# Who issues the stores of rectified chunks: GpSimd in place of SyncE in two passes of a Fourier-layer kernel

## The chip, the cores and the metric

The kernel runs on one core of one Trainium2 chip. The metric is the device time of one execution in microseconds (us). Five runs of the kernel before gave a median of 11392.32 us (11384.97 to 11395.28). The profile is of one further execution, whose own time was 11374.28 us.

## The reference

The model is a tokenizer followed by one transformer layer, for 64 images of 256 x 256 points, all in float32. The tokenizer is a Fourier neural operator with four layers over 32 channels:

```python
v = concat([x, gx, gy]) @ p_w + p_b                  # 3 -> 32 channels
for i in range(4):
    x1 = irfft2(W_i * rfft2(v) on 24 x 12 low modes)   # mixes channels per mode
    x2 = einsum('bcxy,cd->bdxy', v, w_w[i]) + w_b[i]
    v = x1 + x2
    v = (v - mean) * rsqrt(var + 1e-5) * bn_g[i] + bn_b[i]   # statistics over batch, x and y
    if i < 3:
        v = relu(v)
h = squeeze(v @ q_w + q_b)                            # 64 x 256 x 256
h = concat([h, txt], axis=1)                          # 333 tokens of 256
h = h + attention(layernorm(h)); h = h + routed_ffn(layernorm(h))
```

The mean and variance of a layer are over the whole batch, so no image's v can be rectified until the layer's statistics are complete for all 64 images. One full v is 64 images x 8 MiB and does not fit on the core, so it lives in HBM.

## The kernel before

The program has these stages, one after the other: `forward_first` (the low modes of the first v, straight from x), then for each layer i a short stage `mix(i)` (channel mixing per mode, batch statistics), and after the first three of them a long pass `layer(i)`, i = 0, 1, 2. The last layer and the transformer are the tail.

A pass `layer(i)` makes the next v, image by image, in 8 chunks per image. A chunk is a tile of 128 partitions x 8 rows x 256 values, 8 KiB per partition and 1 MiB in all. Its steps are small functions, and each is named by a word:

- `ld` (L632 to L636, passes 1 and 2 alone): loads the chunk of the old v into a tile `vin`, as two halves of 512 KiB (128 partitions x 4 KiB). There are 4 buffers of `vin`. Pass 0 computes its old v from x and loads none.
- `pre`: TensorE adds the inverse transform (L662) and the product of the weights with `vin` (L673) in PSUM (`ring`, four tiles of two banks).
- `evA`, `evB`: each rectifies half of the chunk from PSUM into the tile `vo`, on ScalarE (L685) or VectorE (L687). There are 4 buffers of `vo`.
- `st` (L691 to L694): stores `vo` to HBM, again as two halves of 512 KiB. This is the step that the change touches.
- `turn` (L699) transposes `vo` on VectorE, `prod` (L710) multiplies it by the next layer's weights, and `sqA`, `sqB` (L721) sum squares of that on ScalarE. A `vo` buffer is free for the chunk four later when its store has landed and `turn` and `prod` have read it.
- once per image: `am` loads the mixed modes (`ams`, L603, SyncE's queue) and scales them in place on GpSimd (L611); `sp` and `spT` start the inverse transform from them (L642, L650); `y0` to `y7` (L732), `half`, `zt`, `x` (L766), `xo` make the forward transform of the finished image, and `xs` (L783) stores its modes.

The order is written out by hand. `ORDER` has one string for pass 0 and one for passes 1 and 2: a list of words, each with a chunk number, `@` and an offset of the image, and `.a` or `.d` for the evicting engine. The function `layer` walks through the list once per image and issues the steps under a manual schedule, so each engine gets its instructions in just this order and waits at the first one that is not ready. For passes 1 and 2 it is:

```python
"pre5 sqB7@-1 zt1@-1 sqA7@-1 pre6 evA5.a ld2@1 st4 evB5.d st5 turn4 evA6.a prod5 x@-1 "
"evB6.a sqB5 prod6 sqA5 xo@-1 turn5 pre2@1 sqA6 turn6 sqB6 prod4 evA2.a@1 evB2.d@1 "
"sqB4 ld0@1 ld7 sqA4 pre0@1 evB0.d@1 ld3@1 prod2@1 st6 evA0.a@1 turn2@1 sqB2@1 sqA2@1 "
"pre3@1 ld1@1 evA3.a@1 st2@1 evB3.d@1 pre7 evB7.d prod3@1 ld5@1 evA7.a sqA3@1 turn7 "
"pre1@1 st0@1 am@2 sqB3@1 prod0@1 evA1.a@1 evB1.d@1 sqA0@1 st7 sp1@1 st1@1 ld4@1 y0 "
"spT1@1 y1 ld6@1 turn0@1 turn3@1 xs@-2 y2 sqB0@1 prod1@1 y3 sqB1@1 sp0@2 y4 sqA1@1 "
"spT0@2 y5 y6 st3@1 turn1@1 y7 half.a pre4@1 zt0 prod7 evB4.d@1 evA4.a@1 "
```

Read for one queue alone, this gives SyncE the order ld2, st4, st5, ld0, ld7, ld3, st6, ld1, st2, ld5, st0, am's load, st7, st1, ld4, ld6, xs, st3. GpSimd has in these passes only the scaling of `am`. Where a pass ends, GpSimd issues the next layer's weight loads (`wn`, L387) and the large load of the modes (`xh`, L826).

Of the kernel before, what the change touches and what calls it, by code (L numbers as in the profile page):

```python
# [153 lines left out]
def tile_fno_fusion_transformer(ctx: ExitStack, tc: tile.TileContext, a, cst_d, grid_d, out):  # L154
    nc = tc.nc
# [370 lines left out]
    def layer(i, st, src, dst, acc):  # L526
# [7 lines left out]
        with ExitStack() as cx:  # L534
# [64 lines left out]
            y_, t32, vin, vo, half_, zts = {}, {}, {}, {}, {}, {}  # L599
# [91 lines left out]
            def st_(b, t, e):  # L691
                for n in range(2):
                    rows = slice(4 * n, 4 * n + 4)
                    nc.sync.dma_start(dst[b][:, t, rows], vo[b, t][:, rows])  # L694

            def turn(b, t, e):
                if (b, t // 2) not in t32:
# [84 lines left out]
            def xs(b, n, e):  # L782
                nc.sync.dma_start(xh_d[i][:, b, :], xos.pop(b).rearrange("p g k -> p (g k)"))  # L783

            run = dict(
                am=am, lx=lx, ld=ld, sp=sp, spT=spT, pre=pre, evA=ev(0), evB=ev(1), st=st_, turn=turn,
                prod=prod, sqA=sq(0), sqB=sq(1), y=y, half=half, zt0=zt(0), zt1=zt(1), x=x_, xo=xo, xs=xs,
            )
# [143 lines left out]
    rows = [128, 128, TXT]  # L932
# [283 lines left out]
```

## Time and profile before

| | |
|---|---|
| median of 5 runs | 11392.32 us |
| profiled execution: time, span | 11374.28 us, 11372.5 us |
| granted TensorE clock, mean | 0.976 |
| busy over the span: PE, DVE, ACT, POOL | 93%, 74%, 57%, 13% |
| pass 0, 250 to 2700 us: DMA share, GB/s | 0.71, 248 |
| pass 1, 2900 to 5600 us: DMA share, GB/s | 0.98, 376 |
| pass 2, 5900 to 8500 us: DMA share, GB/s | 0.98, 379 |
| tail, 8900 to 11372 us: DMA share, GB/s | 0.55, 216 |

PE is TensorE's matmuls, DVE VectorE, ACT ScalarE, POOL GpSimd, SP SyncE; SPq and POOLq are the instruction queues from which SyncE and GpSimd issue DMAs. The DMA share is the mean busy share of the core's 16 DMA engines; since packets of different queues can overlap in the records, it can pass 1 for a moment. In the profile a wait is put down to what ended it, and the time "to landing" of a DMA is from its issue to its completion signal, time spent behind other transfers included.

### The profile page before, as it was taken

The numbers are of one execution on the slowest core, as the hardware profiler recorded it, in microseconds if no ns is written. First come the engines' busy times: TensorE is split into PE (matmuls) and PEld (weight loads), VectorE is DVE, ScalarE is ACT, GpSimd is POOL, SyncE is SP. The second block draws the span as 40 slices with busy tenths as digits, with TensorE's granted clock in tenths as the row PEclk, the third lists the DMA queues.
The fourth block names the chain that finished last, engine by engine and source line by source line (L and its number), as shares of the span: only waits on it lengthen the run. The fifth ranks groups of instructions, "written<-read, shape, count | busy, mean of one in ns | idle before, by whom it ended". The sixth has DMA issues, their size and how long they took to land. (4 is left out here: it accounts for less than half of the span.)

```text
span 11372.5 us, 408517 instructions
## 1 busy us (share of the span) xinstructions
PE 10577.0 (93%) x182038; PEld 5726.4 (50%) x182038; DVE 8461.7 (74%) x10405; ACT 6494.3 (57%) x10697; POOL 1477.9 (13%) x2243
## 2 busy tenths in 40 slices
PE   6999999997999999999699999999995999999998
PEld 3555555543444444444344444444443666666666
DVE  6888888886777777777677777777775666666665
ACT  5777777775656656665556665565653333333333
POOL 0111111110000000000100000000001333333333
PEclk7999999998999999999899999999997999999999
DMA  7676676769999999999899999999998555555553
GB/s 235 247 249 245 246 250 247 249 235 327 380 384 380 382 381 376 377 382 381 294 374 384 384 381 378 379 376 376 385 374 272 225 228 228 225 226 227 229 227 135
DMA packets 977151, 3485.52 MB, mean 306 GB/s; under 512 B 151320, under 2 KB 200856, under 8 KB 905368
## 3 DMA queue, kind: packets, MB, share of 16 engines
q1 hardware_dynamic: 906880, 3376.23, 77.6%
q0 software_dynamic: 61360, 79.44, 3.1%
q8 instruction: 1424, 23.33, 0.8%
q10 hardware_dynamic: 7144, 3.72, 0.1%
q14 instruction: 343, 2.81, 0.1%
HBM read 1761.87 MB, written 1696.92 MB: 304 GB/s over the span
## 5 line engine op out<-in xcount | busy, mean ns | idle before, releaser
L721 ACT ACTIVATE ring<-ring 128x1024 f32<-128x1024 f32 x3072 | 3115.9, 1014 | 1178.8 <-PE ring L710 1112.1
L699 DVE STREAM_TRANSPOSE t<-vo 128x2048 f32<-128x2048 f32 x1536 | 3465.4, 2286 | 20.8 <-DVE vo L687 0.5
L710 PE MATMUL ring<-vo,w 32*32 32x512 f32 x49152 | 2404.0, 599 | 82.3 <-ACT vo L685 66.8
L687 DVE TENSOR_SCALAR vo<-ring 128x1024 f32<-128x1024 f32 x1280 | 1545.4, 1222 | 1178.1 <-PE ring L673 801.7
L685 ACT ACTIVATE vo<-ring 128x1024 f32<-128x1024 f32 x1792 | 1791.8, 1023 | 1029.1 <-PE ring L673 489.8
L732 PE MATMUL ring<-t,cst 32*32 32x512 f32 x49152 | 2067.7, 599 | 46.5 <-issue 39.8
L732 PEld LDWEIGHTS ring<-t,cst 32*32 32x32 f32 x49152 | 912.2, 103 | 919.2 <-issue 613.3
L710 PEld LDWEIGHTS ring<-vo,w 32*32 32x32 f32 x49152 | 802.6, 103 | 1062.0 <-issue 397.2
L611 POOL TENSOR_TENSOR ams<-ams,bns 48x512 f32<-48x512 f32 x384 | 401.4, 1045 | 6956.2 <-DMA ams<-mix 6732.7
L662 PE MATMUL ring<-cst,y 24*128 24x256 f32 x16384 | 1228.6, 402 | 74.9 <-DVE vo L687 60.1
L673 PE MATMUL ring<-vin,ws 32*32 32x512 f32 x32768 | 1276.5, 602 | 16.8 <-issue 12.5
L662 PEld LDWEIGHTS ring<-cst,y 24*128 24x128 f32 x16384 | 788.1, 185 | 988.9 <-DVE vo L687 389.6
L650 DVE STREAM_TRANSPOSE y<-ring 128x1024 f32<-128x1024 f32 x384 | 762.9, 1987 | 324.4 <-PE ring L642 323.3
L662 PE MATMUL ring<-mv,y 29*128 29x256 f32 x8192 | 704.2, 403 | 37.2 <-ACT ring L721 19.5
L662 PEld LDWEIGHTS ring<-mv,y 29*128 29x128 f32 x8192 | 455.9, 185 | 368.8 <-ACT ring L721 207.4
L766 PEld LDWEIGHTS ring<-cst,zt 128*128 128x128 f32 x4608 | 532.1, 193 | 178.0 <-ACT vo L685 114.4
L742 ACT COPY half<-ring 128x1024 f32<-128x1024 f32 x192 | 194.4, 1013 | 725.4 <-PE ring L732 725.4
L1165 POOL DMA_DIRECT2D out_dram<-o x1024 | 510.9, 507 | 658.1 <-DVE o L1160 616.5
L721 ACT ACTIVATION_READ_ACCUMULATOR ring<-ring 128x1 f32 x3072 | 585.3, 191 | 0.0
L766 PE MATMUL ring<-cst,zt 128*128 128x96 f32 x4608 | 564.1, 279 | 7.6 <-DVE zt L750 7.2
L750 DVE STREAM_TRANSPOSE zt<-ring 128x1024 f32<-128x1024 f32 x192 | 377.3, 1965 | 242.2 <-PE ring L732 242.2
L642 PE MATMUL ring<-ams,cst 49*128 49x512 f32 (+1 forms) x1536 | 451.8, 642 | 104.3 <-POOL ams L611 38.0
(367 smaller groups left out, 9804.1 us busy)
## 6 DMA issues: line engine op xcount, KB each, us to landing
v<-vo SPq DMA_DIRECT2D x3072, 512.0 KB, 7.8
vin<-v SPq DMA_DIRECT2D x2048, 512.0 KB, 9.1
ch<-v SPq DMA_DIRECT2D x512, 1024.0 KB, 12.7
mix<-ob SPq DMA_DIRECT2D x96, 512.0 KB, 5.7
ams<-mix SPq DMA_DIRECT2D x384, 96.0 KB, 7.9
xin<-in_x_dram SPq DMA_DIRECT2D x16, 1024.0 KB, 6.0
mv<-in_x_dram POOLq DMA_DIRECT2D x256, 64.0 KB, 7.1
out_dram<-o POOLq DMA_DIRECT2D x1024, 16.0 KB, 3.0
```

Source lines behind the costliest of these rows:

```text
L642: nc.tensor.matmul(ps[:, n, :], lhsT=EX[hv, 128 * h:128 * h + 128], rhs=ams[b % 2][hv], start=True, stop=True, skip_group_check=True,)
L650: nc.vector.transpose(y_[b, h].rearrange("p q c -> p c q"), ring[key][0][1].rearrange("p n (c k) -> p (n c) k", k=32),)
L662: nc.tensor.matmul(ps[n][:, 256 * r:256 * r + 256], lhsT=y_[b, t // 4][32 * n:32 * n + K, q:q + 4, :].rearrange("p q c -> p (q c)"), rhs=m ...
L673: nc.tensor.matmul(ps[n][32 * j:32 * j + 32], lhsT=ws[32 * n:32 * n + 32], rhs=v[32 * n:32 * n + 32, 2 * j:2 * j + 2, :], start=False, sto ...
L685: nc.scalar.activation(to, ring[key][h][1], AF.Relu)
L687: nc.vector.tensor_scalar(to, ring[key][h][1], 0.0, None, ALU.max)
L699: nc.vector.transpose(t32[b, t // 2][:, :, 8 * (t % 2):8 * (t % 2) + 8, :].rearrange("p y s c -> p s y c"), vo[b, t].rearrange("p s (y l) ...
L710: nc.tensor.matmul(ps[n][32 * j:32 * j + 32], lhsT=w4[i + 1][32 * n:32 * n + 32], rhs=vo[b, t][32 * n:32 * n + 32, 2 * j:2 * j + 2, :], st ...
L721: nc.scalar.activation(ps, ps, AF.Square, accum_out=acc[:, at:at + 1])
L732: nc.tensor.matmul(ps[n][32 * j:32 * j + 32], lhsT=FYT[32 * n:32 * n + 32, k, :], rhs=t32[b, j][32 * n:32 * n + 32, k].rearrange("p s c -> ...
L766: nc.tensor.matmul(ps[:, 0, 96 * g:96 * g + 96], lhsT=zt_[:, h, k0:k0 + 4, :].rearrange("p k c -> p (k c)"), rhs=FX[:, h, 48 * r:48 * r + ...
L1165: nc.gpsimd.dma_start(out[b, 64 * n + 16 * g:64 * n + 16 * g + 16].rearrange("(p t) d -> p t d", t=2), o[32 * g + 8 * n:32 * g + 8 * n + 8 ...
```

## The change

In passes 1 and 2 (where `i` is not zero) the two half-chunk stores of `st` are issued from GpSimd's queue. In pass 0 they stay with SyncE. The loads `ld`, am's load and `xs` stay with SyncE in all passes. `ORDER`, buffers, sizes and addresses are as they were.

```diff
             def st_(b, t, e):
                 for n in range(2):
                     rows = slice(4 * n, 4 * n + 4)
-                    nc.sync.dma_start(dst[b][:, t, rows], vo[b, t][:, rows])
+                    (nc.gpsimd if i else nc.sync).dma_start(dst[b][:, t, rows], vo[b, t][:, rows])
```

## The prediction

> **What bounds the kernel now.** I read the page's 40 slices first, to see in which stage which resource is full.
>
> ```profile
> PEclk7999999998999999999899999999997999999999
> DMA  7676676769999999999899999999998555555553
> GB/s 235 247 249 245 246 250 247 249 235 327 380 384 380 382 381 376 377 382 381 294 374 384 384 381 378 379 376 376 385 374 272 225 228 228 225 226 227 229 227 135
> ```
>
> Slices 10 to 29 are passes 1 and 2, the only ones that the change touches: DMA stands at 9 tenths or more. The table by stretches of the two passes is sharper (columns: PE, PEld, DVE, ACT, POOL busy; clock; DMA share; GB/s), and the DMA view of the first of them counts the transfers.
>
> ```profile
> 3000.00:5500.00 2500.00, 2399.22 (x51319) 1132.35 (x51306) 1884.92 (x1052) 1508.29 (x2375) 115.06 (x110) 1.00 0.99 380
> 6000.00:8500.00 2500.00, 2394.89 (x51248) 1135.95 (x51251) 1879.83 (x1050) 1509.32 (x2381) 115.03 (x110) 1.00 0.98 379
> ```
>
> ```profile
> vin<-v SPq DMA_DIRECT2D x884, 512.0 KB, 9.1
> v<-vo SPq DMA_DIRECT2D x884, 512.0 KB, 8.8
> ```
>
> 884 half stores are 55.25 images of 16, so an image takes 2500 / 55.25 = 45.2 us. TensorE is busy 2399 / 55.25 = 43.4 us of it and idle 1.8 us. Two resources are nearly full, DMA and TensorE, and neither is quite full. A half chunk at 380 GB/s takes 1.4 us; a store that takes 8.8 us to land has spent most of that behind others. The waits of the same 2500 us, first of SyncE's queue, then of the engines:
>
> ```profile
> SPq L694 <- ACT vo L685: 441.4, 113, 7.3
> SPq L694 <- DMA v<-vo: 296.0, 329, 2.4
> ```
>
> ```profile
> POOL ams L611 <- DMA ams<-mix: 2367.3, 55, 44.7
> ACT vo L685 <- DMA v<-vo: 123.6, 90, 2.7
> DVE vo L687 <- DMA v<-vo: 118.3, 92, 3.1
> ```
>
> So twice per image (113 / 55) SyncE stands 441.4 / 113 = 3.9 us before a store whose chunk is not rectified yet, and whatever loads are behind it stand too. And rectifying waits (123.6 + 118.3) / 55.25 = 4.4 us per image for an old store to land, since its buffer is not free. The order in time of SyncE's queue in one image, and DMA in stretches of 2 us of it:
>
> ```profile
> 4086.80 5.36 SPq L694 DMA_DIRECT2D v<-vo  x4
> 4092.26 3.60 SPq L636 DMA_DIRECT2D vin<-v  x6
> ```
>
> ```profile
> 4086.00:4088.00 2.00, 1.74 (x47) 0.72 (x16) 2.00 (x2) 1.91 (x4) 0.00 (x0) 1.00 0.48 193
> 4088.00:4090.00 2.00, 2.00 (x52) 0.97 (x48) 1.52 (x2) 1.55 (x3) 0.00 (x0) 1.00 1.02 403
> 4090.00:4092.00 2.00, 2.00 (x66) 0.92 (x68) 2.00 (x2) 0.80 (x2) 0.00 (x0) 1.00 0.52 195
> ```
>
> The four half stores are st4 and st5. Until st5 is out at 4092, the six half loads of ld0, ld7, ld3 stand, and the engines run half empty twice: 2 x (0.52 + 0.48) = 2.0 us lost. One image earlier (stretches from 4040 to 4048: 0.91, 1.01, 0.72, 0.91) it is 0.9 us. The mean, 1.45 us per image, is what can be filled.
>
> **The change part by part.**
>
> *Stores leave SyncE.* 2 passes x 64 images x 16 = 2048 DMAs go. The loads behind them issue when a `vin` buffer is free: ld0 needs the buffer that pre5 reads, which ends near 4089.4, three us before its issue at 4092.26. That is the size of the dips. A store also no longer lands behind up to three chunks of loads, so part of the 4.4 us of waiting for `vo` goes. Late next is TensorE, with only 1.8 us of idle time. Gain per image: at least 0 (the dips only move), at most 1.8. I take half of the mean dip, 0.73 us, since stores and loads still share the same engines in the dense half of the image; 0.73 x 128 images = 93 us.
>
> *Stores join GpSimd.* The page's GpSimd rows give the price of an issue:
>
> ```profile
> L618 POOL DMA_DIRECT2D mv<-in_x_dram x256 | 146.6, 576 | 632.2 <-PE ring L662 531.2 <-DVE ams L564 81.3 <-issue 13.5
> L826 POOL DMA_DIRECT2D xh<-xh x3 | 1.7, 566 | 1.9 <-DMA wn<-in_L_tok_fw_dram 1.9
> ```
>
> 16 x 0.57 = 9.1 us per image beside 115 / 55.25 = 2.1 us of scaling: 11.2 of 45.2, hidden in GpSimd's idle time. If it were not hidden it could cost at most the difference to SyncE's 0.32 us at the last chunk of a pass, 0.5 us each.
>
> *Stores queue behind am's wait.* GpSimd now meets st0, then the scaling, which waits for `ams` (8.7 us median to land, then 2.1), then st7, st1, st3. For up to 10.8 us no store can issue. The chunks next rectified are 1, 4, 5, 6; by fours they reuse the buffers of 2, 0, 3, 7. Only 5 and 6 need stores behind the wait, and y0 to y7 (L732, some 11 us of TensorE) lies before them. Cost 0; without that cover up to 10.8 us per image, and below nothing not, since the wait starts nothing earlier. SyncE reaches am's load sooner (st0 no longer before it), so `sp0`, which needs the scaling, is not later.
>
> *The end of a pass.* The next layer's weight loads (L387) stand on GpSimd behind the last two half stores: 2 x 0.57, for 2 passes 2.3 us. With the 1 us above: 3 us.
>
> *Two queues at the engines.* No row shows full-size loads and stores from both. GpSimd's large load alone (4 MB, no other traffic) ran at the engines' full rate:
>
> ```profile
> 5595.00:5604.00 9.00, 0.00 (x0) 0.00 (x0) 1.25 (x2) 1.32 (x2) 1.84 (x4) 0.50 1.04 431
> ```
>
> The other end is pass 0, where GpSimd's 64 KB loads meet SyncE's stores: from 1022 to 1024 the share was 1.05 at 275 GB/s, from 1010 to 1012, without them, 1.02 at 404. Those loads go to 4 partitions each, so they are far from a 128-partition store; the large load is nearer, and I take 0. Ends kept: 431 against 380 would be hidden by TensorE's limit (the 1.8 us); 275 against 404, a third less, would cost about 2000 us.
>
> The sum: -93 + 3 = -90 us. The profiled execution took 11374 us, so 11284; the median of the runs lies 18 us above it: 11302, say 11300.
>
> The row of 0.48 and 0.52 stands against a rule of the Trainium skill. "DMA: Bandwidth & Descriptors", section "Issuing engines are not separate DMA queues", says that all issuers share the same 16 engines and that a second issuer saves only the issue time at the sequencer. By the rule the sum would be about 0 and the time 11392; by the row it is -90, because what SyncE loses is not issue time but waiting in order. The page "SBUF — State Buffer", section "SBUF: two separate sides", speaks against the change too: GpSimd cannot write its descriptors while VectorE runs in a 2-port mode; the VectorE rows of these passes (2283 ns for 2048 values, 1224 for 1024) show about one value per ns, so no doubled rate, and I take no loss from it.
>
> **The rivals.**
>
> *More: TensorE becomes the bound.* If decoupling removes dips and buffer waits wholly, an image takes 43.4 us: 1.8 x 128 = 230 us, 11160. For it: SyncE's 8 us of standing per image. Against: DMA then needs 17 MB in 43.4 us, 395 GB/s, and its best stretches show 400 to 415.
>
> *Same: the dips only move.* The loads go out earlier, land earlier and wait; the engines run dry later in the image, when no buffer is free. 11392, within 23 us (0.2%, about what a measurement of this kernel can tell from no change). For it: the DMA share is already 0.98 to 0.99.
>
> *Slower: packets of two queues get in each other's way.* Loads and stores now alternate at each engine packet by packet. The spare is 1.45 of 45.2 us, 3.2%; from a loss of rate over that it decides. A sixth of the loss seen in pass 0 (a third) is 5.5% of 43.4, or 2.4 us; less the 1.45 filled, +0.95 x 128 = +120 us: 11510. For it: the 275 GB/s row. Against: the 431.
>
> **How the numbers follow.** The forecast (a fill of about half) 0.40, more 0.17, same 0.13, slower 0.30. Faster 0.57, same 0.13, slower 0.30. The likeliest one's own range is 11220 to 11365 (fill of nearly all the dip down to a fifth of it). The 8-in-10 range reaches to TensorE's bound, 11150, and on the other side over half of the slower case, to 11470.
>
> **What would show it.** Right: SyncE's waits at L694 in passes 1 and 2 gone, those for `vin` readers in their place; the dips at st4 and st5 filled; `v<-vo` landing in under 8.8 us from POOLq; "vo <- DMA v<-vo" well below 242 us per 2500; DMA at 385 GB/s or more. Wrong: the same share with fewer GB/s (packets slower); GpSimd's wait for `ams` followed by rectifying that waits for stores; TensorE waiting for `vin` at L673, because loads now share with stores.

## The result and the profile after

The changed kernel took 11369.43 us (median of 25 runs, 11352.93 to 11383.05) beside 11388.43 us for the kernel before (43 runs). The ratio is 0.9984 with a 95% interval of 0.9978 to 0.9989. The gain is 19 us by the medians and 18 us by the ratio (13 to 25). That is a real gain, of the sign forecast, a fifth of the size forecast, and by its middle value within the 0.2% that the prediction called no change, though the interval reaches just past it. The forecast of 11300 us is 69 us too low, and the likeliest case's own range (to 11365) ends 4 us short of the time; the wide range holds it. The profiled execution took 11358.6 us, with a span of 11356.8 us and a granted clock of 0.976, as before.

First the windows of the two passes after the change (columns as in the prediction: PE, PEld, DVE, ACT, POOL busy; clock; DMA share; GB/s), and the DMA view of the first of them.

```profile
3000.00:5500.00 2500.00, 2400.85 (x51311) 1140.32 (x51314) 1885.70 (x1050) 1514.91 (x2385) 581.72 (x996) 1.00 0.98 380
6000.00:8500.00 2500.00, 2402.52 (x51348) 1143.86 (x51342) 1887.81 (x1051) 1512.15 (x2378) 583.88 (x998) 1.00 0.98 380
```

```profile
q1 hardware_dynamic: 142464, 479.19, 51.3%
q0 software_dynamic: 127380, 463.85, 46.1%
vin<-v SPq DMA_DIRECT2D x886, 512.0 KB, 10.3
v<-vo POOLq DMA_DIRECT2D x886, 512.0 KB, 10.2
```

Almost nothing in the first fence moved but POOL. DMA still carries 380 GB/s, and TensorE is still busy 2401 of 2500 us. In the second fence the traffic has become two queues of equal weight, and a store now takes longer to land (10.2 us for 8.8), not less.

The waits of the same window, SyncE's queue and then the engines:

```profile
SPq L636 <- PE ring L673: 1472.3, 381, 13.7
SPq L636 <- DMA vin<-v: 320.6, 210, 3.6
```

```profile
POOL ams L611 <- DMA ams<-mix: 544.7, 52, 12.2
DVE vo L687 <- DMA v<-vo: 106.4, 74, 3.4
ACT vo L685 <- DMA v<-vo: 71.9, 60, 2.4
PEld ring L673 <- DMA vin<-v: 0.7, 2, 0.6
```

SyncE's waits at L694 are gone. It now stands 1472 us of 2500 before a load whose `vin` buffer TensorE is still reading (L673), and 321 us more are put down to an earlier load: no load stands behind a store any more, and the buffers set when most of them go out. GpSimd carries the stores' waits instead:

```profile
POOL v L694 <- ACT vo L685: 1319.0, 330, 12.8
```

Where the dry stretch went is seen in one image of pass 1, in stretches of 2 us, and in the two issuing queues around it:

```profile
4074.00:4076.00 2.00, 2.00 (x65) 0.93 (x68) 1.70 (x2) 0.84 (x2) 0.00 (x0) 1.00 0.68 270
4076.00:4078.00 2.00, 1.74 (x47) 0.72 (x16) 2.00 (x2) 1.91 (x4) 0.53 (x1) 1.00 0.66 145
4078.00:4080.00 2.00, 2.00 (x52) 0.97 (x48) 1.53 (x2) 1.55 (x3) 0.00 (x0) 1.00 0.97 299
```

```profile
4060.00 20.63 SPq L636 DMA_DIRECT2D vin<-v  x6
```

```profile
4063.05 3.21 POOL L694 DMA_DIRECT2D v<-vo  x6
4077.03 0.53 POOL L694 DMA_DIRECT2D v<-vo  x1 [10.76 <-ACT vo L685]
```

From 4066 to 4077 GpSimd has nothing to store, because during `y0` to `y7` TensorE makes no new chunk, so nothing new is rectified. The six half loads of SyncE take 20.6 us to issue for the same reason: no chunk is consumed, so no `vin` buffer comes free. When both have run out, the engines fall to 145 GB/s. Averaged over the middle images of pass 1, GB/s in stretches of 2 us from `sp1`, counted from the trace's packet records:

```
us from sp1   0   2   4   6   8  10  12  14  16  18  20  22  24  26  28  30  32  34  36  38  40  42  44
before      412 412 413 413 415 411 409 414 343 354 267 331 309 297 378 386 357 395 393 411 406 410 414
after       411 405 407 414 413 416 413 342 153 262 331 383 319 354 415 413 415 412 410 416 417 411 411
```

The shallow loss from 16 to 38 us has become a deep one from 14 to 28 us, of the same area: the mean rate is 380 GB/s in both. The equal area shows no more than that an image takes about as long as before, since the bytes are the same. And the deep stretch is no wait of TensorE: its weight loads for L673 waited 0.7 us of 2500 for `vin` (the last row of the waits above), against 12.5 us before.

Last, how long an image takes. The table gives the interval from one image's `sp1` on TensorE to the next one's, in passes that ran the full work (two of before, two of after, and passes of the experiments below). "First" is the first interval of a pass, "later" the mean of the other 62.

| stores of the pass | passes | first, us | later, us (each) | later, mean |
|---|---|---|---|---|
| SyncE, four vin, four vo | 5 | 39.3 to 39.9, mean 39.6 | 45.20, 45.29, 45.43, 45.43, 45.41 | 45.35 |
| GpSimd, four vin, four vo | 4 | 36.6 to 39.0, mean 37.6 | 45.18, 45.24, 45.31, 45.16 | 45.22 |
| the same, `half` moved (see the experiments) | 2 | 38.3, 38.3 | 45.34, 45.14 | 45.24 |
| GpSimd, four vin, five vo | 2 | 36.1, 38.3 | 45.15, 45.21 | 45.18 |
| SyncE, five vin | 2 | 39.7 to 39.9, mean 39.8 | 45.46, 45.36 | 45.41 |
| GpSimd, five vin | 4 | 37.6 to 38.4, mean 38.2 | 45.08, 45.10, 45.17, 45.14 | 45.12 |

The profiled executions of before and after alone (45.20 and 45.29, 45.18 and 45.24) show scarcely any gain per image, since before's was one of its quicker ones; and of the 15.7 us between their two spans, 9.2 lie ahead of the first `sp1` of pass 1, where the change does nothing. Over all the passes of the first two rows the gain is 0.13 us for a later image and 2.0 us for the first: 2 x (62 x 0.13 + 2.0) = 20 us, which agrees with the 18 us measured. The split is rough: the passes of one kind differ by up to 0.23 us for a later image and 2.4 us for the first.

The 2 us at the start of a pass can be seen directly. SyncE's queue where pass 1 begins, before:

```profile
2655.64 4.12 SPq L636 DMA_DIRECT2D vin<-v  x8
2667.60 0.80 SPq L694 DMA_DIRECT2D v<-vo  x2
2668.49 1.98 SPq L636 DMA_DIRECT2D vin<-v  x2
2670.57 9.42 SPq L694 DMA_DIRECT2D v<-vo  x4
```

and after:

```profile
2646.70 48.76 SPq L636 DMA_DIRECT2D vin<-v  x26
```

Before, the fifth chunk's load stood behind the first store of the pass (2667.60), and the next two behind stores that took 9.4 us to issue. After, the first 26 half loads follow one another with no store between them.

### The profile page after: what moved, and what is told of

The parts are those of the page before. It is cut to its first block, busy times and chain, and to the rows that moved or that the text cites. A ratio compares the mean times of both kernels' runs of the same rounds, so it can differ in the third digit from the quotient of the medians.

```text
span 11356.8 us, 408660 instructions
## 1 busy us (share of the span) xinstructions
PE 10568.4 (93%) x182038; PEld 5737.3 (51%) x182038; DVE 8468.0 (75%) x10405; ACT 6499.2 (57%) x10697; POOL 2553.3 (22%) x4291
## 5 line engine op out<-in xcount | busy, mean ns | idle before, releaser
L710 PE MATMUL ring<-vo,w 32*32 32x512 f32 x49152 | 2432.5, 599 | 51.7 <-ACT vo L685 34.2
L732 PE MATMUL ring<-t,cst 32*32 32x512 f32 x49152 | 2099.1, 599 | 60.3 <-issue 53.6
L694 POOL DMA_DIRECT2D v<-vo x2048 | 1086.8, 535 | 3135.7 <-ACT vo L685 3077.9
L732 PEld LDWEIGHTS ring<-t,cst 32*32 32x32 f32 x49152 | 919.4, 103 | 956.4 <-issue 641.2
L710 PEld LDWEIGHTS ring<-vo,w 32*32 32x32 f32 x49152 | 817.6, 103 | 1024.4 <-issue 447.5
L662 PE MATMUL ring<-cst,y 24*128 24x256 f32 x16384 | 1225.4, 401 | 110.3 <-DVE vo L687 85.9
L662 PEld LDWEIGHTS ring<-cst,y 24*128 24x128 f32 x16384 | 784.0, 184 | 1025.3 <-DVE vo L687 421.0
L673 PE MATMUL ring<-vin,ws 32*32 32x512 f32 x32768 | 1235.6, 601 | 10.3 <-issue 10.0
L662 PE MATMUL ring<-mv,y 29*128 29x256 f32 x8192 | 705.0, 403 | 37.0 <-ACT ring L721 20.1
L662 PEld LDWEIGHTS ring<-mv,y 29*128 29x128 f32 x8192 | 455.9, 185 | 369.0 <-ACT ring L721 211.6
## 6 DMA issues: line engine op xcount, KB each, us to landing
vin<-v SPq DMA_DIRECT2D x2048, 512.0 KB, 10.2
```

The costliest lines, as they stand in the source:

```text
L662: nc.tensor.matmul(ps[n][:, 256 * r:256 * r + 256], lhsT=y_[b, t // 4][32 * n:32 * n + K, q:q + 4, :].rearrange("p q c -> p (q c)"), rhs=m ...
L673: nc.tensor.matmul(ps[n][32 * j:32 * j + 32], lhsT=ws[32 * n:32 * n + 32], rhs=v[32 * n:32 * n + 32, 2 * j:2 * j + 2, :], start=False, sto ...
L694: (nc.gpsimd if i else nc.sync).dma_start(dst[b][:, t, rows], vo[b, t][:, rows])
L710: nc.tensor.matmul(ps[n][32 * j:32 * j + 32], lhsT=w4[i + 1][32 * n:32 * n + 32], rhs=vo[b, t][32 * n:32 * n + 32, 2 * j:2 * j + 2, :], st ...
L732: nc.tensor.matmul(ps[n][32 * j:32 * j + 32], lhsT=FYT[32 * n:32 * n + 32, k, :], rhs=t32[b, j][32 * n:32 * n + 32, k].rearrange("p s c -> ...
```

## The experiments

Two theories stood against each other at first. By one, DMA and its dry stretches hold the image: with less to move it falls to TensorE's 43.4 us, and the change gained little because it filled little. By the other, TensorE's order with its hand-overs holds it: transfers that start earlier, or fewer of them, move it little. The letters A, B and so on belong to each expectation as it words them. Every kernel below starts from before or from the changed kernel, as its diff says.

### Less to store, stores on SyncE

```diff
-                for n in range(2):
+                for n in range(1 if i == 2 else 2):
```

> The kernel before (all stores on SyncE), but pass 2 stores only the first half of each chunk: 512 of its 1024 half stores, a quarter of its traffic, are left out; pass 1 is as it was and serves as control. Theory A (an image is held by its transfers, as the prediction's sum had it): pass 2's image falls from 45.2 us to TensorE's busy time of 43.4, the whole by some 115 us to 11275. Theory B (TensorE's order of work with its hand-overs to the evicting engines holds the image at 45.2, and transfers have room in it): pass 2's image stays within 0.3 us of 45.2, the whole within 25 us of the kernel before.

Measured, one execution of each: 11327.2 us beside 11403.37 on the same chip. A later image of pass 2 took 44.30 us, and of the untouched pass 1 45.43. Pass 2's window:

```profile
6000.00:8300.00 2300.00, 2228.62 (x48180) 1085.81 (x48176) 1772.83 (x987) 1423.64 (x2233) 108.69 (x104) 1.00 0.81 293
```

With a quarter of the traffic gone the DMA share falls to 0.81, yet the image loses only some 1.1 us, between the fall to 43.4 us and the standstill that were expected. TensorE still stands 2300 - 2229 us over 2300 / 44.3 images, 1.4 us per image, of the 1.8 us that it stood before. So most of the idle time on which the forecast drew is not DMA's: it lies in hand-overs that lighter DMA leaves as they are. The rest of the 1.1 us came out of TensorE's busy time, which fell to 2229 / 51.9 = 42.9 us per image, so the 43.4 us of the prediction are no fixed floor.

### The same with stores on GpSimd

```diff
-                for n in range(2):
+                for n in range(1 if i == 2 else 2):
                     rows = slice(4 * n, 4 * n + 4)
                     (nc.gpsimd if i else nc.sync).dma_start(dst[b][:, t, rows], vo[b, t][:, rows])
```

> The changed kernel with only the first half of each chunk stored in pass 2 (the other half is not written, so DMA there has a quarter less to move); stores on GpSimd in passes 1 and 2. Theory A (an image is held by TensorE's order with its hand-overs, some 44.3 us once DMA is light, whichever engine issues the stores): pass-2 image 44.3 us, as when SyncE issued the halved stores. Rival D (GpSimd's issue itself slows the work, which is why the steady image gained nothing): over 44.7 us. Rival E (SyncE's waits cost TensorE something even with light DMA): 43.4 to 43.9 us.

Measured, in one execution: 11299.56 us beside 11386.91. A later image of pass 2 took 44.10 us.

```profile
6000.00:8300.00 2300.00, 2225.61 (x48369) 1075.92 (x48368) 1779.71 (x991) 1426.77 (x2242) 329.21 (x520) 1.00 0.81 294
```

Theory A held: 44.1 us with GpSimd as issuer, 44.3 with SyncE, not 43.4. Under light DMA an image ends near 44.2 us whoever issues the stores; a gain as small as the 0.13 us of the change can't be told apart here, as the two single executions differ by 0.2 us. A quarter less traffic brings some 1.1 us per image, so a change of issuer, which moves as many bytes as before, could hardly have brought 0.73.

### Less for TensorE, then both, then with the change

The y steps 1 to 6 go in pass 2; the second kernel takes the halved stores of the first experiment as well, and the third puts the same cut into the changed kernel:

```diff
             def y(b, k, e):
                 if k == 0:
                     take(("y", b), 2)
+                if i == 2 and 0 < k < 7:
+                    return
```

> The kernel before, but pass 2 leaves out steps 1 to 6 of the eight forward-transform steps y (6/8 of the 10.5 us of L732 per image, 7.9 us of TensorE); all transfers stay. Theory A: pass 2's image stays at 45.2, DMA at 380 GB/s. Theory B: it falls until DMA is really full, 17.2 MB at the 413 GB/s of the best stretches, 41.6 us and a little idle: about 42.5 us, the whole by 170 us to 11220.

> The kernel before with both left out in pass 2: half of the stores and steps 1 to 6 of y. Theory A: the image goes to the larger of 3/4 of 45.2 (33.9) and TensorE's busy rest 43.4 - 7.9 = 35.5 us: 35.5, the whole by 620 us. Theory B: 45.2 - 7.9 = 37.3 us, the whole by 505 us to 10885.

> The changed kernel (stores of passes 1 and 2 on GpSimd), with steps 1 to 6 of y left out in pass 2 as in the run before it. If the split removes the dry stretches of DMA once TensorE no longer holds the image, pass 2's image is some 1 us shorter than with all on SyncE (the mean dip is 1.45 us): 41.5 against 42.5. If the dry stretches only move, the two are equal within 0.3 us.

Measured, one execution of each: 11286.74, 11140.71 and 11258.03 us beside 11403.37. A later image of pass 2 took 43.95, 41.57 and 43.54 us. Pass 2's window of each, in this order:

```profile
6000.00:8300.00 2300.00, 2112.18 (x38572) 912.12 (x38571) 1763.50 (x994) 1429.90 (x2256) 108.64 (x104) 0.91 1.00 390
```

```profile
6000.00:8300.00 2300.00, 2097.02 (x40820) 935.92 (x40815) 1862.36 (x1053) 1519.91 (x2384) 117.04 (x112) 0.97 0.86 312
```

```profile
6000.00:8300.00 2300.00, 2033.45 (x38889) 902.65 (x38900) 1776.62 (x1005) 1444.73 (x2269) 557.82 (x952) 0.95 1.01 394
```

The first and the third of these are spoiled as a measure of TensorE's share. With its work cut TensorE stands still for a stretch of each image, and the granted clock then falls for the matmuls after it. Two stretches of one image of the first kernel show it (the clock stands third from the end):

```profile
7032.00:7034.00 2.00, 0.56 (x1) 0.46 (x2) 2.00 (x2) 1.78 (x3) 1.88 (x2) 0.87 1.02 418
7034.00:7036.00 2.00, 2.00 (x4) 0.49 (x2) 1.08 (x1) 0.36 (x2) 0.21 (x1) 0.50 1.04 424
```

The second, with both cut, keeps a clock of 0.97 and still lies over 4 us above what either theory gave it: TensorE stands 2300 - 2097 us over 55.3 images, 3.7 us per image, with DMA at 0.86. Its busy time was 2097 / 55.3 = 37.9 us per image, not the 35.5 reckoned. Neither resource is full and the image is still not at TensorE's busy time, which speaks for the order with its hand-overs but does not prove it. What can be read from the other two is that DMA does become the limit once TensorE has less to do: a share of 1.00 at 390 GB/s with stores on SyncE, 394 on GpSimd, with the image 0.4 us shorter in the latter. Two queues at once cost no rate. Part of the 0.4 us may be the clock (0.95 for 0.91), so the two outcomes named for the third kernel, 1 us or nothing, are not decided.

### The start of a pass and the rest, apart

```diff
-                    nc.sync.dma_start(dst[b][:, t, rows], vo[b, t][:, rows])
+                    (nc.gpsimd if i and b < 2 else nc.sync).dma_start(dst[b][:, t, rows], vo[b, t][:, rows])
```

and with `b >= 2` in place of `b < 2` for the other part.

> The change for images 0 and 1 of passes 1 and 2 alone; from image 2 on the stores are SyncE's again. If the measured gain of the change (19 us) lies in the start of a pass, where SyncE's loads of the second half of image 0 stand behind its first stores (the first image takes 3.3 and 2.2 us less in the changed kernel), this keeps most of it: 8 to 19 us less than before. If the gain is spread over the images (0.15 us each), it is within 5 us of before.

> The converse: images 0 and 1 of passes 1 and 2 store from SyncE, all later ones from GpSimd. If the gain lies in the start of a pass: within 6 us of before. If it is spread: 12 to 19 us less.

Measured: the first two images alone 11381.39 us (ratio 0.9993, 0.9984 to 1.0002), all but the first two 11382.23 us (0.9994, 0.9985 to 1.0003), beside 11393.26. The intervals are too wide to say how the 18 us divide by time alone. The traces agree with the table above: with the first two images on GpSimd the first interval is 38.4 and 38.3 us and later ones are 45.39 and 45.37; with all the others it is 39.5 and 39.7 us, and 45.26 and 45.28. Both parts seem to gain and neither is the whole, but neither gain is clear of noise by itself.

### Five buffers for the rectified chunks

On the changed kernel; `half` moves into a tile that is free by then, to make room.

```diff
-                for n, k in (("lo", 4), ("ly", 1), ("lc", 1), ("lx", 2), ("lz", 1), ("lt", 6))
+                for n, k in (("lo", 5 if i else 4), ("ly", 1), ("lc", 1), ("lx", 2), ("lz", 1), ("lt", 6))
-                    half_[b] = zp.tile([128, 2, 512], F32, name="half")
+                    half_[b] = t32[b, 0].rearrange("p y s c -> p (y s c)")[:, 0:1024].rearrange("p (n q) -> p n q", n=2)
```

> The changed kernel with five buffers of vo in place of four in passes 1 and 2 (the ScalarE copy `half` goes into the already read first quarter of t32 in place of a tile of its own, which makes the room). Theory C (TensorE with its evictions could do an image in 44.3 us, DMA in 44.0, and only the few buffers, which let DMA run dry before pre4, tie the two into 45.2): the image falls to 44.3 to 44.8, the whole by 50 to 110 us to some 11290. Theory B (TensorE's order alone makes 45.2): no change, within 15 us of the changed kernel.

Measured: 11371.46 us, ratio 0.9981 (0.9972 to 0.999), no better than the change alone, as theory B had it. Its waits of rectifying for stores:

```profile
ACT vo L685 <- DMA v<-vo: 28.4, 18, 3.0
DVE vo L687 <- DMA v<-vo: 20.6, 26, 2.5
```

49 us of 2500 are left, of 242 before and 178 after the change, and the time did not follow. So what was left of the 4.4 us per image that the prediction read from these rows was not on the path.

### A fifth vin buffer, with and without the change

On the changed kernel, and then on the kernel before; in both `half` moves as above, and a third kernel moves `half` alone on the changed kernel.

```diff
-            ip = pool("li", 2 if i == 0 else 4, reuse_waits="tile")
+            ip = pool("li", 2 if i == 0 else 5, reuse_waits="tile")
```

> The changed kernel with five buffers of vin in place of four, with the same room made. Theory C: one more chunk can be under way while TensorE does y0 to y7, so the dry stretch of DMA shrinks by up to 2.6 us and the image falls to 44.3 to 44.8, the whole by 50 to 110 us. Theory B: within 15 us of the changed kernel.

> The kernel before (all stores on SyncE) with five vin buffers in place of four in passes 1 and 2; the half of the z stage lies in t32 to make room. Theory A (the fifth vin buffer is worth about 18 us by itself, because loads run further ahead of TensorE whoever issues the stores): 0.3% below the kernel before. Rival B (a fifth vin buffer can only be filled once the loads no longer stand behind the stores' waits on SyncE): within 0.1% of the kernel before. Rival C (the gain of the kernel with five vin and split stores came from the new place of half): as A, but then the run with the half's new place alone shows it too.

> The changed kernel with only the half of the z stage moved into t32, four vin and four vo buffers as before. Theory A (the buffer counts decide): equal to the changed kernel, 0.9984 of the kernel before. Rival C (the half's place was the gain): 0.997 of the kernel before.

> The changed kernel with five vin buffers, the half in t32: the same kernel as the run with five vin before, for an interval beside the two others. If the gain was real: 0.9967 of the kernel before, some 18 us under the changed kernel. If it was chance of a few runs: 0.9984.

| kernel | median, us | ratio to before | interval |
|---|---|---|---|
| change and five vin | 11351.34 | 0.9967 | 0.9952 to 0.9981 |
| the same again | 11349.48 | 0.9963 | 0.9950 to 0.9976 |
| five vin, stores on SyncE | 11383.12 | 0.9998 | 0.9988 to 1.0007 |
| change, `half` moved | 11377.13 | 0.9991 | 0.9981 to 1.0000 |

The fifth buffer is worth nothing by itself (rival B of that run) and some 20 us beyond the change once the stores are out of the way (28 us beside the kernel with `half` moved). That is less than the 50 us at least that theory C asked for and more than theory B allowed. The place of `half` is not the gain. Why the buffer needs the change is in SyncE's waits. Five `vin` with stores on SyncE:

```profile
SPq L694 <- ACT vo L685: 460.3, 129, 7.7
SPq L694 <- DMA v<-vo: 299.0, 326, 2.1
SPq L636 <- PE ring L673: 9.1, 23, 0.5
```

and with stores on GpSimd:

```profile
SPq L636 <- PE ring L673: 1648.4, 384, 16.3
```

In the first, a load almost never meets a full `vin` (9 us of 2500): the stores ahead of it in the queue hold it longer than the buffers do, so a further buffer is filled no sooner. In the second it is mostly the buffers that hold it. How the fifth buffer gains its 20 us is not shown: the dry stretch is still there (148 GB/s from 16 to 18 us after `sp1` in pass 1, 153 with four), DMA carries 380 GB/s as before, and a later image is shorter by 0.10 to 0.12 us, which makes 12 to 15 us over the two passes. Change and five `vin` together, 11349 us, are the best kernel of this study, 0.37% below before.

## Why the prediction was right or wrong

*What bounds the kernel.* Right that both DMA and TensorE are nearly full. Wrong in what the 1.8 us of TensorE's idle time is. After the change TensorE still stands 1.8 us per image (99 us over 55.4 images), and with a quarter of the traffic gone 1.4 us.

*Stores leave SyncE: the step that failed.* The prediction put -93 us there, 0.73 us per image, half of the mean dip. Measured is 0.13 us per image, 16 us over the two passes, and some 4 us more at their starts, on which the prediction had not reckoned. Its mechanism happened: L694's waits left SyncE, readers of `vin` took their place, and loads went out earlier. What failed is the price: the prediction took time in which DMA runs below its rate for time that TensorE loses. TensorE's own waits in the same 2500 us of the kernel before, the largest of its matmuls' and the one of its weight loads for `vin`, are these:

```profile
PE ring L662 <- DVE vo L687: 24.9, 97, 0.5
PEld ring L673 <- DMA vin<-v: 12.5, 22, 1.3
```

Of the 101 us in which TensorE's matmuls stood, 57 ended with a hand-over from an engine that rectifies (L662 above, and L710 and L642 for ScalarE's `vo`), and 0.4 us with a load. Its weight loads, which overlap the matmuls, waited 12.5 us for one, in pass 2's window 6.8. Together that is at most 0.23 us per image to be had by earlier loads, not 0.73 (with 7.5 us of rectifying put down to a load and 9.0 us of the same weight loads put down to a store it would be 0.53). After the change 0.7 and 2.1 us are left of the 12.5 and 6.8.

The dips themselves moved, and so did the time of the image on TensorE. The mean of the middle images, from the first matmul of one step to that of the next, in the passes of the first two rows of the table:

| stretch of an image | SyncE, us | GpSimd, us | difference |
|---|---|---|---|
| `sp1` to `pre4` (the y steps) | 13.44 | 13.79 | +0.35 |
| `pre4` to `pre6` | 6.59 | 6.51 | -0.08 |
| `pre6` to the next image's `pre3` | 14.91 | 15.21 | +0.30 |
| `pre3` to `sp1` | 10.41 | 9.70 | -0.71 |

Each of these differences is larger than the spread between the passes of one kind (0.16 us at most), except the second. So 0.71 us were gained in one part of the image, about the size forecast, and 0.57 lost in the others. That is the rival "Same" in mechanism, to which the prediction gave 0.13; its own sentence for it was that the engines run dry "when no buffer is free" (it said later in the image; it is at the end of the y steps, ahead of the old dip). But what TensorE lost is no wait for a load: the y steps read no `vin`, and L673 waits less than before. The trace of before held the sign of it: 1.45 us per image were read from two images, as if a dip filled at one place had no price elsewhere, while DMA's share over 2500 us was already 0.98 to 0.99.

*The wait for `vo`.* Counted as part of the gain, since 4.4 us per image were shown. It fell to 178.3 / 55.4 = 3.2 us with the change and to 0.9 us with five `vo`, and neither shows in the time. It lay beside TensorE's other work.

*What slows the y steps* stays open. The cadence of neighbouring matmuls, from the trace (gaps over 0.4 us left out):

```
ns from one matmul's start to the next    L732 (y)   L710 (prod)   L673 (pre)
before, pass 1                              31.44       29.11         18.83
after, pass 1                               32.08       29.82         18.44
half stores on SyncE, pass 2                32.02       29.23         18.25
```

With 256 matmuls of each line per image, after against before is +0.16, +0.18 and -0.10 us. It is no chance of one trace: in the steady part of every pass with full traffic the busy time of L732 is 10.6 to 10.7 us per image with the stores on SyncE and 10.8 to 10.9 with them on GpSimd. The third row shows the slower y steps without any store on GpSimd, so its issuing is not what they need. No run here goes further.

*Stores join GpSimd.* Right: the issue was costed at 0.57 us and took 535 ns on average, hidden.

```profile
L694 POOL DMA_DIRECT2D v<-vo x2048 | 1086.8, 535 | 3135.7 <-ACT vo L685 3077.9
```

*Stores queue behind am's wait.* Right that it happens and costs nothing that can be seen. GpSimd stands up to 12.2 us for `ams`, and 2.2 us of scaling follow (the prediction said up to 10.8 with the scaling), and the six half stores of one image then go out together (4063.05, x6, above) while the y steps run.

*The end of a pass.* +3 us was not resolved: from the last `sp1` of pass 1 to the first of pass 2 it is 188.3 us before and 189.3 after, and such gaps lie anywhere from 185.5 to 190.0 us in the kernels whose last stores of pass 1 are SyncE's, as before.

*Two queues at the engines.* Right at 0, and the rival "Slower" is out: 380 GB/s at a share of 0.98 as before, and a packet of 4096 bytes took 168 ns on average in both (162 on GpSimd's queue, 174 on SyncE's after). Packets of full-size loads and stores do not get in each other's way here; so pass 0's 275 GB/s was no guide to them. The 0 was luck in part: the transfers of the row of 431 GB/s on which it leaned came in packets of 21 KB on average (4.63 MB in 221 packets, 5594 to 5606 us), not of 4096 bytes.

*More: TensorE becomes the bound.* Out: 43.4 us per image was not reached even with half the stores of a pass left out (44.1).

*The rule of the Trainium skill* that the prediction weighed and set aside ("DMA: Bandwidth & Descriptors", "Issuing engines are not separate DMA queues") came nearer than the row: by it 11392, by the row 11302, measured 11369. What was gained at the start of a pass is not issue time but order: four stores, of some 0.32 us each to issue, held SyncE's queue for 9.42 us (2670.57, above). The other one ("SBUF — State Buffer", "SBUF: two separate sides") did not bite: of 1339 us for which GpSimd's stores waited in 2500, 1319 are for ScalarE's rectifying, and the issue took 535 ns.

*The signs.* Gone from SyncE at L694: yes. "vo <- DMA v<-vo" below 242: yes, and worth nothing. Dips at st4 and st5 filled: yes, but dug anew earlier in the image. Landing under 8.8 us: no, 10.2; why was not tested. DMA at 385 GB/s or more: no, 380. This last was the one that carried the gain, and it is the one to have doubted. Of the signs of being wrong, GpSimd's wait for `ams` came, but rectifying waited less for stores than before (178 us for 242), not more; the GB/s did not fall; and TensorE waited less for `vin`, not more.

## What to carry to other kernels

Before giving a dry stretch of DMA a price, look for the engine on the path that waits for its transfers: here DMA ran below its rate for microseconds per image, but TensorE's waits for loads came to some 0.2 us per image. Then ask which buffer a freed transfer will land in, since a load that meets a full buffer goes out no sooner. Taking the stores out of the loads' queue and giving the loads one more buffer were worth 18 us and nothing apart, and some 40 us together; count such edits together, since one hides the other's limit. A short dip found in two images is not a mean; the table of one long window, with its DMA share of 0.98, was the better guide.

## What the runs showed of the hardware that I had not expected

- Leaving out six of the eight y steps cost clock: where TensorE stood for a stretch in each image, the granted clock went to 0.50 for the matmuls after it and to 0.91 over the pass (1.00 with full work). With DMA at a share of 1.00 in that pass, what this cost can't be told apart.
- Loads and stores of 512 KiB issued from two queues at once carried the same 380 GB/s as from one, 394 GB/s where TensorE held them less (390 from one queue), and 410 to 417 in the dense part of each image.
- The cadence of TensorE's matmuls shifted by 2% with nothing changed in their own instructions or in the granted clock (31.44 to 32.08 ns in L732, 18.83 to 18.44 in L673). I can't say why.
